# Two transformer layers on one core: one slotted pipeline over both layers in place of two separate ones

## Chip, cores and metric

The kernel runs on one core of one Trainium2 chip. The metric is the device time of one execution in microseconds (us), as the median of several runs. The core has a matrix engine (PE, with its weight loads shown as PEld), a vector engine (DVE), an activation engine (ACT), a general engine (POOL) and a queue for transfers (SP). ACT and POOL can issue transfers too.

## What is computed

Input is x with 16 x 64 = 1024 tokens of 512 features, and a context of the same shape. All is float32. Four residual steps follow one another:

```
x = x + L0_attention(layernorm(x), ctx)      # 32 heads of 128, 8 kv heads, rotary, tanh-capped logits, key mask
x = x + L0_experts(layernorm(x))             # 4 low-rank experts, the best 2 per token, softmax gate
x = x + L1_attention(layernorm(x), ctx)      # 16 heads of 96, 4 kv heads, keys = context and x of the same batch
x = x + L1_linear(layernorm(x))              # x W^T + bias + 16 weighted low-rank updates
```

Attention is within a batch of 64 tokens: a query sees 64 context keys in layer 0, and 64 context plus 64 own keys in layer 1. So a token tile of 128 (two batches) depends on no other tile, except through the weights that all share.

## The kernel before

x stays in eight SBUF tiles xt[0..7] of 128 tokens. hT (L149) holds the context and the normalised x, both transposed, features on the partitions. "Half" means 512 tokens, that is four of the tiles.

`layernorm_T` (L192) normalises all eight tiles in two groups of four: statistics on DVE, square root on ACT, normalising on DVE, four PE transposes a tile into a PSUM tile with tag "pa", and a copy by ACT to hT. It is called four times, ahead of each of the four steps, each time over all tokens.

A layer 0 unit (`l0_unit`, L241) is a kv head and a half. Its **chunks** make the projections: one k chunk (L267), four q chunks (L277), and on every other kv head, in half 0 only, four v chunks for both kv heads and all tokens (L289). A k or q chunk is four matmuls of 128 x 512 (eight PE records, since a float32 matmul shows as two) and then the rotation `rope` (L245): two ACT copies that swap the halves, a product on DVE, one on POOL, a sum on DVE. The projections take PSUM tiles of tag "pa", of which there are two, as the transposes do. Its two **items** are 256 tokens each and go through four stages:

- `l0_scores` (L318): scores on PE, tanh and exp on ACT, mask on POOL (L338, L341)
- `l0_norm` (L346): row sums on PE (sm, L349), reciprocal on DVE (L351), product on POOL (en, L353)
- `l0_av` (L356): weights times values on PE (av, L365), four copies by ACT (at, L374)
- `l0_wo` (L379): two output products on PE (po, L386), each added to a tile xt by DVE (L393)

Layer 1 (`l1_unit`, L510) has the same form: kv head and half, two k chunks (none for the last kv head), three q chunks, eight v chunks for kv head 0, and four items of 128 tokens with the stages `l1_scores` (L581: maximum on DVE, four exponentials on ACT, scaling on POOL), `l1_transpose` (L611: four PE transposes and a DVE copy eT), `l1_av` (L619) and `l1_wo` (L639). Scores, sums and transposes share two PSUM tiles of tag "pb"; av has two of tag "pc", outputs two of tag "pd".

The order is written by `_run_pipeline` (L71), once per layer. In its step n it emits scores of item n, then the second stage of item n-1, the third of n-2, the fourth of n-3, and between these stages the chunks of the next unit, spread over the unit's items. Units follow kv head by kv head, both halves of each. So four items are in work at a time, and a layer's last outputs come three steps after its last scores. The framework that builds the program sets the semaphores and may place ready instructions of an engine in another order than the code's.

Between the two pipelines stands the code of the experts (L440 to L502), with a norm ahead of it and one behind. After the second pipeline come the loads of the last step's weights, their merge (L667 to L674: the low-rank updates multiplied out and added to W), a norm, the bias adds on POOL (L677) and the linear product (pf, L681) with its output transfers.

At the start SP's queue loads the eight x tiles (L145) and then weights, POOL's queue the whole context in one transfer of 2 MB (L150), ACT's queue the small tables. Weight tiles have two buffers per tag; `load_w0` for the next kv head is called with the first chunk of a unit, `load_wo0` after the last.

Of the kernel before, what the change touches and what calls it, by code (L numbers as in the profile page):

```python
# [70 lines left out]
def _run_pipeline(units, lag_stages):  # L71

    n_st = len(lag_stages)
    for f in units[0][0]:
        f()
    flat = [(u, it) for u, (_, items) in enumerate(units) for it in items]  # L80
    states = []
    pending, done_in_unit = [], 0
    for n in range(len(flat) + n_st - 1):
        take = []
        if n < len(flat):
            u, it = flat[n]
            per_unit = len(units[u][1])
            if n % per_unit == 0:
                pending = list(units[u + 1][0]) if u + 1 < len(units) else []
                done_in_unit = 0  # L90
            k = -(-len(pending) // (per_unit - done_in_unit))
            take, pending = pending[:k], pending[k:]
            done_in_unit += 1
            states.append(it)
        cuts = [len(take) * i // n_st for i in range(n_st + 1)]
        spread = [take[cuts[i] : cuts[i + 1]] for i in range(n_st)]
        for s in range(n_st):
            m = n - s
            if 0 <= m < len(flat):
                lag_stages[s](states[m])  # L100
            for f in spread[s]:
                f()
# [3 lines left out]
def two_layer_kernel(  # L106
# [35 lines left out]
    xt = []  # L142
    for i in range(NT):
        t = const.tile([P, D], F32, tag=f"x{i}", name=f"x{i}")
        nc.sync.dma_start(out=t, in_=x[ts(i, P), :])  # L145
        xt.append(t)


    hT = const.tile([P, 2, KC, NTOK], F32, tag="hT", name="hT")  # L149
    nc.gpsimd.dma_start(out=hT[:, 0], in_=ctxT.rearrange("(c p) n -> p c n", p=P))  # L150

    ident = const.tile([P, P], F32, tag="ident", name="ident")
    make_identity(nc, ident)
    blk = const.tile([P, P], F32, tag="blk", name="blk")
    nc.vector.memset(blk, 0.0)
    nc.vector.memset(blk[0:S, 0:S], 1.0)
    nc.vector.memset(blk[S:P, S:P], 1.0)
    eps_c = const.tile([P, 1], F32, tag="eps", name="eps_c")
    nc.vector.memset(eps_c, EPS)
    cos_sb = const.tile([P, S], F32, tag="cos", name="cos_sb")  # L160
    sin_sb = const.tile([P, S], F32, tag="sin", name="sin_sb")
    nc.scalar.dma_start(out=cos_sb, in_=cos)
    nc.scalar.dma_start(out=sin_sb, in_=sin)


    mask_w = const.tile([P, S // 4], I32, tag="mask_w", name="mask_w")
    for j in range(2):
        nc.scalar.dma_start(out=mask_w[j * S : (j + 1) * S, :], in_=maskT)
    keep = const.tile([P, S], F32, tag="keep", name="keep")
    nc.vector.tensor_copy(keep, mask_w.bitcast(U8))  # L170
    cnt = ps.tile([P, S], F32, tag="pb", name="cnt")
    nc.tensor.matmul(cnt, lhsT=blk, rhs=keep, start=True, stop=True)

    none_kept = const.tile([P, S], F32, tag="none_kept", name="none_kept")
    nc.vector.tensor_scalar(none_kept, cnt, 0.0, None, ALU.is_equal)


    tri = const.tile([P, NE, NE], F32, tag="tri", name="tri")
    nc.vector.memset(tri, 0.0)
    for e in range(1, NE):  # L180
        nc.vector.memset(tri[:, e, 0:e], 1.0)

    bias_bc = const.tile([P, D], F32, tag="bias", name="bias_bc")
    nc.scalar.dma_start(out=bias_bc, in_=bias1.partition_broadcast(P))
    w_er = const.tile([P, 2], F32, tag="w_er", name="w_er")
    sc_er = const.tile([P, 2], F32, tag="sc_er", name="sc_er")
    nc.scalar.dma_start(out=w_er, in_=coeffs)
    nc.scalar.dma_start(out=sc_er, in_=scales)
    nc.vector.tensor_mul(w_er, w_er, sc_er)


    def layernorm_T():  # L192
        for grp in range(2):
            tiles = range(grp * 4, grp * 4 + 4)
            mv = small.tile([P, 4, 2], F32, tag="mv", name="mv")
            for n, i in enumerate(tiles):
                st = small.tile([P, 6], F32, tag="st", name="st")
                nc.vector.bn_stats(st, xt[i])
                nc.vector.bn_aggr(mv[:, n, :], st)
            rstd = small.tile([P, 4], F32, tag="rstd", name="rstd")  # L200
            nc.scalar.activation(rstd, mv[:, :, 1], AF.Sqrt, bias=eps_c)
            nc.vector.reciprocal(rstd, rstd)
            for n, i in enumerate(tiles):
                xn = work.tile([P, D], F32, tag="xn", name="xn")
                nc.vector.tensor_scalar(
                    xn, xt[i], mv[:, n, 0:1], rstd[:, n : n + 1], ALU.subtract, ALU.mult
                )
                tp = ps.tile([P, KC, P], F32, tag="pa", name="tp")
                for c in range(KC):
                    nc.tensor.transpose(tp[:, c, :], xn[:, ts(c, P)], ident)  # L210
                nc.scalar.copy(hT[:, 1, :, ts(i, P)], tp)
# [4 lines left out]
    def load_w0(kv):  # L216
        wq = wp.tile([P, KC, G0 * HD0], F32, tag="wq", name="wq")
        nc.sync.dma_start(
            out=wq, in_=wq0[:, ts(kv, G0 * HD0)].rearrange("(c p) n -> p c n", p=P)
        )  # L220
        wk = wp.tile([P, KC, HD0], F32, tag="wk", name="wk")
        nc.sync.dma_start(out=wk, in_=wk0[:, ts(kv, HD0)].rearrange("(c p) n -> p c n", p=P))
        if kv % 2 == 0:
            wv = wp.tile([P, KC, 2 * HD0], F32, tag="wv", name="wv")
            nc.sync.dma_start(
                out=wv, in_=wv0[:, ts(kv // 2, 2 * HD0)].rearrange("(c p) n -> p c n", p=P)
            )
        else:
            wv = w0[kv - 1][2]
        w0[kv] = [wq, wk, wv]  # L230

    def load_wo0(kv):
        wo = wp.tile([P, G0, D], F32, tag="wo", name="wo")
        nc.sync.dma_start(
            out=wo, in_=wo0[ts(kv, G0 * HD0), :].rearrange("(g p) n -> p g n", p=P)
        )
        w0[kv].append(wo)
# [3 lines left out]
    def l0_unit(kv, half):  # L241
# [62 lines left out]
        def first():  # L304
            if half == 0 and kv + 1 < KV0:
                load_w0(kv + 1)
            k_chunk()

        chunks = [first]
        if half == 0 and kv % 2 == 0:  # L310
            chunks += [lambda n=n: v_chunk(n) for n in range(4)]
        chunks += [lambda g=g: q_chunk(g) for g in range(G0)]
        if half == 0:
            chunks.append(lambda: load_wo0(kv))
        items = [{"unit": unit, "quad": qd} for qd in range(2)]
        return chunks, items
# [62 lines left out]
    def l0_wo(it):  # L379
# [14 lines left out]

    load_w0(0)
    layernorm_T()
    _run_pipeline(
        [l0_unit(kv, half) for kv in range(KV0) for half in range(2)],
        [l0_scores, l0_norm, l0_av, l0_wo],
    )  # L400

# [3 lines left out]
    nc.sync.dma_start(out=aw, in_=aw0.rearrange("(c p) n -> p c n", p=P))  # L405
    bcat = const.tile([P, D], F32, tag="bcat", name="bcat")
    for j in range(2):
        nc.sync.dma_start(out=bcat[j * NM : (j + 1) * NM, :], in_=b0)
# [21 lines left out]
    load_w1(0)  # L430
    wv1s = []
    for m in range(2):
        wv = wp.tile([P, 2, KV1 * HD1], F32, tag="wv", name="wv1_sb")
        nc.sync.dma_start(
            out=wv, in_=wv1[ts(m, 2 * P), :].rearrange("(c p) n -> p c n", p=P)
        )
        wv1s.append(wv)
    layernorm_T()

    for grp in range(2):  # L440
# [50 lines left out]
        gmf = gm.rearrange("p n e r -> p (n e r)")  # L491
# [13 lines left out]
    layernorm_T()  # L505
    v1 = [act.tile([P, B // 2, KV1 * HD1], F32, tag="v", name=f"v1_{h}") for h in range(2)]
# [3 lines left out]
    def l1_unit(kv, half):  # L510
# [19 lines left out]
        def first():  # L530
            if half == 0 and kv + 1 < KV1:
                load_w1(kv + 1)
            if kv < PK1:
                unit["k"] = act.tile([HD1, nb, 2, S], F32, tag="k", name="kT1")
            else:
                unit["k"] = k_last[:, half * nb : (half + 1) * nb]
            unit["q"] = act.tile([HD1, nb, G1, S], F32, tag="q", name="qT1")
            if kv < PK1:
                k_chunk(0)
# [37 lines left out]
        if half == 0:  # L577
            chunks.append(lambda: load_wo1(kv))
        return chunks, [{"unit": unit, "pair": pr} for pr in range(nb // 2)]
# [59 lines left out]
    def l1_wo(it):  # L639
# [11 lines left out]
        nc.vector.tensor_add(xt[i], po, xt[i])  # L651

    _run_pipeline(
        [l1_unit(kv, half) for kv in range(KV1) for half in range(2)],
        [l1_scores, l1_transpose, l1_av, l1_wo],
    )

# [73 lines left out]
```

## Time and profile before

| | us |
|---|---|
| median of 3 runs | 1098.24 |
| lowest and highest | 1092.36, 1098.29 |
| the profiled execution | 1091.64 |
| its span in the trace | 1089.9 |
| PE busy | 1053.4 |
| DVE, ACT, POOL busy | 429.3, 318.0, 292.9 |

The span runs from the first to the last recorded instruction; the execution's own time is 1.7 us longer. The stretches between the stages, by the rows of PE in order of time:

| from, to (us) | what PE does |
|---|---|
| 0 to 18.4 | waits for x, apart from one small product |
| 18.4 to 25.9 | first norm's transposes |
| 25.9 to 60.5 | k, v and q of the first unit, k of the second |
| 60.5 to 683.4 | layer 0 items and chunks |
| 683.4 to 690.9 | norm |
| 690.9 to 718.9 | experts |
| 718.9 to 725.9 | norm |
| 725.9 to 1045.8 | layer 1 |
| 1045.8 to 1052.7 | merge |
| 1052.7 to 1061 | norm, with first linear products |
| to 1086.0 | linear; the last output lands near the end of the span |

A busy share is of the whole span. Matmuls are pipelined, so the records of neighbours overlap: 597 ns is the record of one 512-column record, 0.43 us the distance between two. "Idle before" names what the engine waited for last.

### The profile page before, as it was taken

Reading aid. Unit: us, or ns where it says so; the run is one execution under the profiler, and the core shown is the slowest. Engines: PE = TensorE matmul, PEld = TensorE weight load, DVE = VectorE, ACT = ScalarE, POOL = GpSimd, SP = SyncE. Lnnn points to the kernel's source line nnn. Section 1 sums busy time; section 2 is a strip of 40 time slices with the busy share of each in tenths; the row PEclk is TensorE's granted clock in tenths of the full one; section 3 lists DMA queues with packets and bytes.
Section 4 is the critical chain, followed back from the end, with each engine's and each line's share of the span. In section 5 each row is a group of like instructions: output and inputs, shape, how many; then the busy total and the mean of one; then the engine's idle time right before and its main releaser. Section 6 shows DMA issues by size and latency. Waiting matters only on the chain.

```text
span 1089.9 us, 9279 instructions
## 1 busy us (share of the span) xinstructions
PE 1053.4 (97%) x3398; PEld 535.4 (49%) x3398; DVE 429.3 (39%) x639; ACT 318.0 (29%) x835; POOL 292.9 (27%) x257
## 2 busy tenths in 40 slices
PE   3999999999999999999999999789999999999998
PEld 2644455444455444455444444545555555556543
DVE  4145433343433343433344445540123334334661
ACT  2243322232322232222232221231433433333420
POOL 0155422243432243332243341002220111111140
PEclk9999999999999999999999999879999999999999
DMA  9210011011011011011011010000010010010002
GB/s 334 78 42 7 10 39 58 10 39 39 10 39 53 10 39 38 11 39 53 11 29 39 10 58 1 29 0 1 11 49 0 1 59 1 29 39 20 1 1 77
DMA packets 26142, 38.57 MB, mean 35 GB/s; under 512 B 2288, under 2 KB 12528, under 8 KB 26096
## 3 DMA queue, kind: packets, MB, share of 16 engines
q1 hardware_dynamic: 24688, 35.53, 9.8%
q0 software_dynamic: 528, 2.10, 0.5%
q8 instruction: 27, 0.44, 0.2%
q10 hardware_dynamic: 880, 0.34, 0.1%
q14 instruction: 19, 0.16, 0.0%
HBM read 35.87 MB, written 2.10 MB: 35 GB/s over the span
## 4 chain that ended last, share of the span: by engine, by line
PE 95%; DVE 2%; DMA 1%; ACT 1%; issue 0%; POOL 0%; ACTq 0%; DVEq 0%; POOLq 0%
PE pq L280 21%; PE po L386 20%; PE pq L544 8%; PE po L644 7%; PE pv L295 5%; PE pk L272 5%; PE pk L518 4%; PE pv L562 4%; PE av L365 3%; PE sm L349 3%; PE sc L324 3%; PE sc L586 3%; PE av L624 2%; PE pf L681 2%; PE tp L210 1%; PE tp L614 1%
## 5 line engine op out<-in xcount | busy, mean ns | idle before, releaser
L280 PE MATMUL pq<-hT,wq 128*128 128x512 f32 x512 | 231.5, 597 | 0.0
L386 PE MATMUL po<-wo,at 128*128 128x512 f32 x512 | 226.1, 594 | 0.0
L259 POOL TENSOR_TENSOR w<-sh,sin_sb 128x512 f32<-128x512 f32 x80 | 102.7, 1284 | 312.5 <-ACT sh L250 312.2
L386 PEld LDWEIGHTS po<-wo,at 128*128 128x128 f32 x512 | 96.4, 190 | 119.6 <-issue 118.5
L280 PEld LDWEIGHTS pq<-hT,wq 128*128 128x128 f32 x512 | 95.5, 190 | 119.0 <-issue 117.6
L351 DVE RECIPROCAL r<-sm 128x512 f32<-128x512 f32 x32 | 107.4, 3357 | 47.2 <-PE sm L349 44.3
L249 ACT COPY sh<-pq 64x512 f32<-64x512 f32 x64 | 37.2, 582 | 296.2 <-PE pq L280 296.2
L252 DVE TENSOR_TENSOR u<-pq,cos_sb 128x512 f32<-128x512 f32 x64 | 44.0, 688 | 156.4 <-ACT sh L250 156.4
L608 POOL TENSOR_TENSOR e<-e,sm 128x512 f32<-128x512 f32 x32 | 33.2, 1039 | 220.5 <-DVE sm L607 220.5
L393 DVE TENSOR_TENSOR x<-po,x 128x512 f32<-128x512 f32 x64 | 44.2, 690 | 120.5 <-PE po L386 118.1
L644 PE MATMUL po<-wo_sb,at 128*128 128x512 f32 x192 | 87.5, 592 | 0.0
L544 PE MATMUL pq<-hT,wq_sb 128*128 128x512 f32 x192 | 86.0, 592 | 0.0
L338 POOL TENSOR_TENSOR e<-e,keep 128x512 f32<-128x512 f32 x32 | 40.5, 1267 | 92.0 <-ACT e L337 91.7
L265 DVE TENSOR_TENSOR qT<-u,w 128x512 f32<-128x512 f32 x64 | 45.2, 706 | 35.6 <-POOL w L259 35.3
L599 ACT ACTIVATE e<-sc,nmx 128x128 f32<-128x128 f32 x128 | 45.2, 365 | 47.5 <-DVE nmx L595 44.4
L544 PEld LDWEIGHTS pq<-hT,wq_sb 128*128 128x128 f32 x192 | 36.2, 190 | 43.9 <-issue 42.6
L272 PE MATMUL pk<-hT,wk 128*128 128x512 f32 x128 | 57.6, 593 | 0.1
L295 PE MATMUL pv<-wv,hT 128*128 128x256 f32 x256 | 57.2, 380 | 0.0
L353 POOL TENSOR_TENSOR en<-e,r 128x512 f32<-128x512 f32 x32 | 47.5, 1485 | 23.6 <-DVE r L351 15.4
L295 PEld LDWEIGHTS pv<-wv,hT 128*128 128x128 f32 x256 | 48.4, 190 | 10.4 <-issue 3.6
L644 PEld LDWEIGHTS po<-wo_sb,at 128*128 128x128 f32 x192 | 36.3, 190 | 33.8 <-issue 29.9
L552 DVE COPY qT<-pq 96x512 f32<-96x512 f32 x24 | 16.5, 687 | 87.7 <-PE pq L544 87.7
(105 smaller groups left out, 1099.7 us busy)
## 6 DMA issues: line engine op xcount, KB each, us to landing
wq<-in_wq SPq DMA_DIRECT2D x8, 1024.0 KB, 5.5
wo<-in_wo SPq DMA_DIRECT2D x8, 1024.0 KB, 5.3
wq_sb<-in_wq SPq DMA_DIRECT2D x4, 768.0 KB, 4.7
wo_sb<-in_wo SPq DMA_DIRECT2D x4, 768.0 KB, 4.6
x<-in_x SPq DMA_DIRECT2D x8, 256.0 KB, 6.2
hT<-in_ctxT POOLq DMA_DIRECT2D x1, 2048.0 KB, 13.0
wk<-in_wk SPq DMA_DIRECT2D x8, 256.0 KB, 4.1
wv<-in_wv SPq DMA_DIRECT2D x4, 512.0 KB, 5.1
```

The lines of the kernel that those rows point to most:

```text
L259: nc.gpsimd.tensor_tensor(w.rearrange("p (b t) -> p b t", t=S), sh.rearrange("p (b t) -> p b t", t=S), sin_b, ALU.mult,)
L265: nc.vector.tensor_tensor(dst, u, w, ALU.add)
L272: nc.tensor.matmul(pr, lhsT=w0[kv][1][:, c, :], rhs=hT[:, 0, c, tok], start=c == 0, stop=c == KC - 1)
L280: nc.tensor.matmul(pr, lhsT=w0[kv][0][:, c, ts(g, HD0)], rhs=hT[:, 1, c, tok], start=c == 0, stop=c == KC - 1,)
L295: nc.tensor.matmul(pr[:, i, :], lhsT=hT[:, 0, c, ts(2 * n + i, P)], rhs=w0[kv][2][:, c, :], start=c == 0, stop=c == KC - 1,)
L351: nc.vector.reciprocal(r, sm)
L353: nc.gpsimd.tensor_tensor(en.rearrange("p a t -> p (a t)"), ef, r, ALU.mult)
L386: nc.tensor.matmul(po, lhsT=it["at"][:, g, ts(pr, P)], rhs=wo[:, g, :], start=g == 0, stop=g == G0 - 1,)
L393: nc.vector.tensor_add(xt[i], po, xt[i])
L544: nc.tensor.matmul(pr, lhsT=w1s[kv][0][:, c, ts(g, P)], rhs=hT[:, 1, c, ds(half * HALF, HALF)], start=c == 0, stop=c == KC - 1,)
L599: nc.scalar.activation(e[:, n, :], sc[:, n, :], AF.Exp, bias=nmx[:, n : n + 1], scale=SCALE1, accum_out=sm[:, n : n + 1],)
L644: nc.tensor.matmul(po, lhsT=it["at"][:, g].rearrange("d m t -> d (m t)"), rhs=w1s[u["kv"]][2][:, g, :], start=g == 0, stop=g == PK1 - 1,)
```

## The change

`_run_pipeline` goes. `_run(items, fillers)` takes one list of items over both layers and a table of other work by time slot:

```
SLOTS = 4
LAG = 2

def _run(items, fillers):
    last = max([SLOTS * (len(items) - 1) + LAG * 3, *fillers])
    for t in range(last + 1):
        for m in range(len(items)):
            s, odd = divmod(t - SLOTS * m, LAG)
            if not odd and 0 <= s < 4:
                items[m]["stages"][s](items[m])
        for f in fillers.get(t, []):
            f()
```

An item starts every four slots, and its stages are two slots apart: scores at 4m, the second stage at 4m+2, the third at 4m+4, the fourth at 4m+6. In a slot the stages are emitted first, the earlier item ahead, and then the slot's fillers. So at slot 4m stand the third stage of item m-1 and scores of m, at 4m+2 the fourth of m-1 and the second of m.

The order of units is changed so that half 0 ends before half 1, and the chunks of each unit are spread over the slots of the one before (8 slots in layer 0, 16 in layer 1):

```
    units0 = [(kv, half) for kv in range(KV0 - 2) for half in range(2)]
    units0 += [(kv, half) for half in range(2) for kv in (KV0 - 2, KV0 - 1)]
    units1 = [(kv, half) for k2 in range(0, KV1, 2) for half in range(2) for kv in (k2, k2 + 1)]
...
    def spread(a, b, work):
        for n, f in enumerate(work):
            put(a + (b - a) * n // len(work), f)
...
    for a, b in zip(units0, units0[1:]):
        if b != (0, 1):
            spread(begin[0, a], begin[0, b], built0[b][0] + built0[b][1])
```

`layernorm_T` becomes `ln_stats(*tiles)` and `ln_tile(i)`, the experts `experts_mid(grp)` and `experts_out(grp)`, for one half each. They are put at slots counted from the last output of a half:

```
    for half, t in ((0, h0), (1, h1)):
        at = (2, 3, 6, 7, 8) if half == 0 else (2, 4, 8, 9, 11)
        normed = [lambda i=i: ln_tile(i) for i in halves[half]]
        put(t, lambda half=half: ln_stats(*halves[half]))
        put(t + at[0], *normed)
        put(t + at[1], lambda half=half: experts_mid(half))
        put(t + at[2], lambda half=half: experts_out(half))
        put(t + at[3], lambda half=half: ln_stats(*halves[half]))
        put(t + at[4], *normed)
    spread(h0 + 9, u0, built1[0, 0][0])
    spread(u0, begin[1, (1, 0)], built1[1, 0][0])
    spread(h1 + 12, u1, built1[0, 1][0])
    for a, b in zip(units1[2:], units1[3:]):
        spread(begin[1, a], begin[1, b], built1[b][0])
```

With 16 layer 0 units the slots are: half 0 of layer 0 ends at h0 = 114 while units (6, 1) from 112 and (7, 1) from 120 are in work; layer 1 begins at u0 = 128; half 1 ends at h1 = 130; u1 = 160; the last unit begins at 240.

The end of layer 1 is treated in the same way. The merge is cut into four calls `merge(c)`, the linear step into `linear(i)` with the bias add of its tile:

```
    put(begin[1, (2, 0)], load_updates)
    put(begin[1, (2, 1)], load_w, weigh_updates)
    put(begin[1, (3, 1)], *[lambda c=c: merge(c) for c in range(KC)])
    put(h0, lambda: ln_stats(*halves[0]))
    put(begin[1, (3, 1)] + 2, *[lambda i=i: ln_tile(i) for i in halves[0]])
...
    put(h1 - 5, stats(4, 5))
    put(h1 - 4, applied(0), normed(4))
    put(h1 - 3, stats(6), normed(5), applied(1))
    put(h1 - 2, applied(2))
    put(h1 - 1, normed(6), applied(3))
    put(h1, stats(7), applied(4), applied(5), normed(7), applied(6), applied(7))
    _run(items, fillers)
```

The start is rewritten. The context comes in eight transfers on SP's queue (a half is four of 128 x 512), x on ACT's queue, the small tables on POOL's. Weights of the first kv head are loaded in parts, in the order k, v, q:

```
    load_small()
    load_w0(0, 0)
    load_ctx(0)
    load_w0(0, 1)
    for i in range(NT):
        nc.scalar.dma_start(out=xt[i], in_=x[ts(i, P), :])
    load_ctx(1)
    load_w0(0, 2)
    make_identity(nc, ident)
    constants()
    load_wo0(0)
    load_w0(1)
    for f in built0[0, 0][0]:
        f()
    ln_stats(*halves[0])
    for f in built0[0, 1][0]:
        f()
    for i in halves[0]:
        ln_tile(i)
    mask_constants()
    ln_stats(*halves[1])
    for f, i in zip(built0[0, 0][1], halves[1]):
        f()
        ln_tile(i)
    spread(0, begin[0, (0, 1)], built0[0, 1][1])
```

Here built0[u][0] are the k and v chunks of a unit and built0[u][1] its q chunks. The later weight loads become fillers too:

```
    for kv in range(2, KV0):
        put(begin[0, (kv - 1, 0)] - (8 if kv > 2 else 0), lambda kv=kv: load_w0(kv))
    for kv in range(1, KV0):
        put(max(begin[0, (kv, 0)] - 2, 0), lambda kv=kv: load_wo0(kv))
    put(begin[0, (5, 0)], load_experts, load_late)
...
    put(begin[0, (7, 0)], load_wv1)
    put(begin[0, (6, 1)], lambda: load_w1(0))
    put(begin[0, (7, 1)] + 2, lambda: load_w1(1))
    put(begin[0, (7, 1)] + 6, lambda: load_wo1(0))
    put(u0 + 4, lambda: load_wo1(1))
```

The bodies of the chunks and of the stages, the tiles, their buffers and the number of bytes loaded are the same as before.

## The prediction

> **What bounds the kernel now.** I read the busy times first, then the table of windows by stage, then the chain that ended last, then the rows of the two stretches between the layers in order of time.
>
> ```profile
> PE 1053.4 (97%) x3398; PEld 535.4 (49%) x3398; DVE 429.3 (39%) x639; ACT 318.0 (29%) x835; POOL 292.9 (27%) x257
> ...
> PE 95%; DVE 2%; DMA 1%; ACT 1%; issue 0%; POOL 0%; ACTq 0%; DVEq 0%; POOLq 0%
> ```
>
> PE carries the end: 97% busy, 95% of the chain. The windows say where the other 3% lies (columns: length, then busy time of PE, PEld, DVE, ACT and POOL, granted clock, DMA share, GB/s):
>
> ```profile
> 0.00:20.00 20.00, 2.30 (x10) 2.07 (x10) 8.19 (x32) 2.03 (x4) 1.67 (x7) 1.00 0.94 322
> 40.00:640.00 600.00, 600.00 (x1804) 282.32 (x1802) 240.74 (x240) 171.88 (x347) 220.70 (x169) 1.00 0.09 29
> 640.00:720.00 80.00, 67.98 (x246) 34.42 (x246) 45.84 (x100) 16.91 (x37) 10.66 (x9) 0.88 0.08 30
> 720.00:1060.00 340.00, 337.49 (x1199) 190.14 (x1197) 124.15 (x254) 119.46 (x436) 55.95 (x70) 0.99 0.05 17
> ...
> 640.00:650.00 10.00, 8.73 (x28) 3.64 (x28) 5.00 (x5) 1.98 (x5) 5.58 (x5) 1.00 0.21 79
> ...
> 710.00:720.00 10.00, 6.11 (x12) 2.59 (x12) 8.17 (x21) 0.30 (x1) 0.00 (x0) 0.50 0.00 0
> ```
>
> Over 600 us of layer 0 PE has no gap at all, so nothing can be won there and every new wait is paid in full. What can be won is at the ends. I counted PE's work at full pace from undisturbed rows: a chunk of 8 matmul records (q, k, one wo output) takes 3.43 us from start to next start, scores+sums+av of a layer 0 item 3.34, a layer 1 item 4.77 (score to score where no chunk lies between), one token tile's transposes 0.44. Layer 0: (80 chunks + 64 outputs) x 3.43 + 16 v chunks x 3.45 + 32 x 3.34 = 656. Layer 1: 36 chunks x 3.43 + 41.3 of v + 32 x 4.77 = 317. Norm tiles 32 x 0.44 = 14, experts 14.6, merge and linear 80 records x 0.43 = 34. Sum 1036 of the 1089.9 us span; 54 are slack. They lie so. **Head**: the first scores start at 60.49 after 37.9 of work: 22.6. **Middle**: 1.3 before scores at 641.65; first norm (683.4 to 690.9) 7.5 less 3.5 = 4.0; experts (690.9 to 718.9) 28.0 less 14.6 = 13.4, at half clock for most of it; second norm 6.9 less 3.5 = 3.4: together 22. **End**: last norm 2.3, output 3.9. The rest is small.
>
> **The change part by part.** Matmuls, copies, vector work and bytes stay the same in number; order, queues and lags change.
>
> *Head, -6 (2 to 9).* x goes from SP's queue to ACT's; the context, one 2 MB transfer on POOL's queue (13.0 us to landing beside x), becomes eight on SP, the first half behind 0.25 MB of wk. The same table in steps of 2 us sums to 2.7 MB moved by 10 us and 4.3 by 14. With equal shares, the first k chunk has its 1.25 MB when 2.5 have moved, 9.5 us; wv comes at 3.5 MB, 12 us. So v0 starts at 12.5, v0 to v3 and the second k chunk end near 30; four tiles at 0.85 each (their pace in the head, two PSUM buffers behind a 0.59 us copy) 33.5; then four q chunks, each followed by one tile. Both take a buffer of the same pair; a q chunk's is free only 2.1 us after its end (two copies of 0.58, product of 0.69), the tile's 0.8 after its 0.44, so about 0.8 of PE wait per chunk: 4 x 4.7 = 19. Scores near 54 instead of 60.5. The small tables move to POOL's queue (four issues near 1 us), due for the first rotation after 10 us: hidden, and 1 to 2 us late at worst.
>
> *Middle, -19 (12 to 22).* Half 0's norms and experts fall among the last layer 0 units, half 1's among the first layer 1 units. Their waits (copies 0.59, the gate's chain of some 20 short DVE operations, 4.3 us) lie beside items, and the clock should stay up. 22 less some 3 for tiles that queue on the two PSUM buffers.
>
> *End, -2.* Merge and half 0's linear run inside the last unit, so PE has 3 linear tiles (10.3) to cover the last tile's chain: add 0.69, statistics 0.86, square root 0.3, normalising 0.55, transposes, copy, together about 4.6. The 3.9 of output stay. Bias adds (1.27 on POOL) hide beside each 3.43.
>
> *Weight loads, 0.* SP waits in order, each load on the last reader of its buffer. Each is placed behind that reader and about a unit (37 us) ahead of use, against 5.5 us to landing. If one came late, PE would lose up to those 5.5.
>
> *Short lags in layer 0, +40 (0 to 43).* Before, sums and av of an item were a whole item (18 us) apart. Now sums sit at slot 4m+2, av at 4m+4, and a unit without v chunks puts its five chunks at slots 0, 1, 3, 4, 6: one chunk, 3.43, between sums and av. The chain is shown here (start, duration, engine, line, operation, in brackets idle before):
>
> ```profile
> 638.19 1.14 PE L365 MATMUL av<-en,v 64*128 64x256 f32 x8
> ...
> 639.26 1.13 PE L386 MATMUL po<-wo,at 128*128 128x512 f32 x2
> ...
> 641.65 1.08 PE L324 MATMUL sc<-qT,kT 128*64 128x256 f32 x8 [1.27 <-DVE qT L265]
> ...
> 642.67 1.13 PE L349 MATMUL sm<-e,blk 128*128 128x512 f32 x2
> ...
> 643.63 6.17 PE L386 MATMUL po<-wo,at 128*128 128x512 f32 x14
> ...
> 643.83 3.36 DVE L351 RECIPROCAL r<-sm 128x512 f32<-128x512 f32 x1 [2.23 <-PE sm L349]
> ...
> 647.27 1.26 POOL L353 TENSOR_TENSOR en<-e,r 128x512 f32<-128x512 f32 x1 [0.54 <-DVE r L351]
> ```
>
> Sums start at 642.67, en is ready at 648.53: 5.86, and 6.2 where POOL's en takes its usual 1.58. PE has 0.96 + 3.43 = 4.39 to do. So av waits 1.5 to 1.8, say 1.65, and behind it in PE's queue stand the next scores, the next chunk and wo. Of 32 items, six have v chunks beside them (two chunks, 6.9) and the last two layer 1's first chunks: 24 x 1.65 = 40. The lower bound is 0, because PE's order isn't the code's:
>
> ```profile
> 56.94 3.60 PE L272 MATMUL pk<-hT,wk 128*128 128x512 f32 x8
> 60.49 1.08 PE L324 MATMUL sc<-qT,kT 128*64 128x256 f32 x8
> ```
>
> The code emits these scores ahead of this k chunk; the program was built with the chunk first, since q's rotation wasn't ready. If the builder foresees the reciprocal's 3.36 as well, it slips the next scores and a matmul or two in. No row shows that. The nearest row is the 1.27 above: same layer, a 3.4 us chain, and the built order still came 1.27 too early. The chain here is 5.1 behind the sums; I take the full 1.65.
>
> *Short lags in layer 1, +5 (0 to 38), table loads, +3.* Scores to transposes takes 5.2 to 6.0 (maximum 0.69, four exponentials 1.5, scaling on POOL 1.04); with no chunk in that half of an item PE has scores and wo, 3.46. In code order ten items would wait 1.75 or more and fourteen would wait 1.2 for the transposed copy: 35 to 38. Here rows do show the builder filling in (scores, a piece of a k chunk, scores, at 763.8), and what stayed was 0.60, 0.19 and 0.24 in the last items:
>
> ```profile
> 1030.28 1.06 PE L586 MATMUL sc<-k_last,qT 96*128 96x128 f32 x8
> ...
> 1036.30 0.66 PE L614 MATMUL tp<-ident,e 128*128 128x128 f32 x4 [0.24 <-POOL e L608]
> ```
>
> I take 0.35 at some 15 handoffs. Norms between items make square root and exponential alternate: about 8 more table loads. The row has 1283 ns for one, and the next ACTIVATE 1.30 after its start. [...] Three pairs fall where layer 1's chain has little cover: 3 x 2.6 = 7.7 by the row[...]. [...] count 3 because chunks cover the rest.
>
> *Clock under many short waits, 0.* [...] 710 to 720, waits near 3 us, clock 0.50; 640 to 650, one wait of 1.27, clock 1.00. By the row 24 waits cost nothing more[...]. I take the row.
>
> **Sum.** 1089.9 - 6 - 19 - 2 + 40 + 5 + 3 = 1111 span. The profiled run was 1091.64, 1.7 above its span; the median of the runs, 1098.24, is 6.6 above that, the lowest 1092.36 near it. I add 1.7 and 1.5: 1114.
>
> **Rivals.** *The order hides the lags, faster.* One mechanism, at sums to av: the next scores (0.97) and two matmuls of the next chunk (1.7) go ahead of av. Then 1089.9 - 27 + 4 = 1067 span, 1070 with what lies around it. For it: 56.94 above, and no PE gap in 600 us. Against: 641.65. It decides when the wait per item is under 0.6. *Gain given back, no change.* The builder covers half: 20 instead of 40, giving 1091 span, 1094. For it: waits of 0.2 to 0.6 in layer 1's tail. *The change doesn't do what it says*: the middle stays a gap because half 1's chain (some 35 us) runs out of other work; but the first two layer 1 units hold 38 us of items and 17 of chunks, so this loses at most a few us, and ends within the other cases.
>
> **How the numbers follow.** Paid lags 0.45 (1106 to 1124), half covered 0.24 (1084 to 1104), covered 0.31 (1064 to 1082). Layer 1 at its upper bound is inside the first one's top. The range 1068 to 1124 leaves out the fringes. 1% is about what a measurement of this kernel tells from no change; the cases fall on its sides, so slower 0.45, within 0.24, faster 0.31.
>
> **What would show it.** Right: PE's waits list av L365 <- POOL en some 24 times at 1.5 to 1.8, PE below 600 in layer 0's 600 us, the stretch between the layers without a clock drop, first scores near 54. Wrong: PE still gapless in layer 0 with scores or half chunks between sums and av; or head and middle keeping their slack; or the clock falling below 1.00 among the items.

## The result and the profile after

The changed kernel takes 1128.86 us (median of 4 runs, 1124.95 to 1128.89) against 1095.3 us of the kernel before (4 runs, 1091.26 to 1098.29): 1.030 times as long, 95% interval 1.025 to 1.035. It is slower, as forecast, but lies beyond the forecast's upper end of 1124. The profiled execution spans 1127.0 us, 37.1 more than before.

From the page of the changed kernel, first the busy times, then the chain that ended last:

```profile
PE 1062.4 (94%) x3398; PEld 533.3 (47%) x3398; DVE 434.8 (39%) x641; ACT 324.9 (29%) x843; POOL 287.0 (25%) x263
...
PE 77%; DVE 9%; POOL 6%; ACT 4%; issue 3%; DMA 1%; POOLq 0%; ACTq 0%; DVEq 0%
```

PE has the same 3398 records, but no longer the chain: 95% before, 77% now. VectorE and GpSimd, 2% of the old chain together, carry 15%: their chains are no longer covered. The windows by stage of the changed kernel say where (columns as before: length, busy PE, PEld, DVE, ACT, POOL, granted clock, DMA share, GB/s):

```profile
0.00:20.00 20.00, 10.64 (x30) 5.67 (x31) 9.35 (x31) 3.09 (x6) 5.83 (x14) 1.00 0.93 322
40.00:640.00 600.00, 568.38 (x1698) 269.13 (x1697) 227.76 (x224) 159.51 (x325) 195.44 (x155) 1.00 0.08 26
640.00:720.00 80.00, 73.51 (x222) 33.09 (x221) 42.26 (x66) 21.20 (x41) 22.55 (x19) 0.89 0.08 24
720.00:1060.00 340.00, 334.25 (x1188) 182.94 (x1187) 125.79 (x261) 118.94 (x403) 49.98 (x65) 1.00 0.07 21
```

PE starts earlier (10.6 us of work in the first 20 against 2.3), but the 600 us from 40 to 640, gapless before, now hold 568.4; about 6 of the 31.6 that are missing lie ahead of the first scores at 65.80, the rest in layer 0. And from 640 to 720 the clock is 0.89, as low as before (0.88), though the old gap between the layers is full of work.

For the account I laid both traces out alike: the length of a stretch less PE's work in it at full pace, with the paces the prediction used. This is loss, by idling or by half clock. The count works with mean paces, so a line is good to about 1.5 us.

| stretch | loss before | loss after | change | forecast |
|---|---|---|---|---|
| head, to the first scores | 21.5 | 25.5 | +4.0 | -6 |
| layer 0, to the first norm between the layers | 2.7 | 33.5 | +30.8 | +40 |
| between the layers, to the last norm tile of half 1 | 24.1 | 21.4 | -2.7 | -19 |
| layer 1 | -0.9 | 2.1 | +3.0 | +5 and +3 |
| end, from about the last unit | 6.6 | 10.1 | +3.5 | -2 |

The changes sum to 38.6, where the spans differ by 37.1; the 1.5 between them is the error of the count, since both traces hold the same 3398 records, kind by kind. PE's waits in the changed kernel (us in total, times, longest):

```profile
PE sc L318 <- DVE qT L266: 14.7, 15, 1.3
PE av L359 <- POOL en L347: 12.9, 22, 2.1
PE pk L273 <- DMA hT<-in_ctxT: 7.1, 3, 6.2
PE pq L281 <- ACT hT L203: 6.6, 5, 1.5
```

Only the first was in the list before, with 1.3 us. The forecast had named the second, as 24 waits of 1.5 to 1.8. One unit of layer 0 in the changed kernel, in order of time, shows both:

```profile
129.71 1.02 PE L343 MATMUL sm<-e,blk 128*128 128x512 f32 x2
130.57 3.60 PE L281 MATMUL pq<-hT,wq 128*128 128x512 f32 x8
134.00 1.02 PE L273 MATMUL pk<-hT,wk 128*128 128x512 f32 x2
135.59 1.13 PE L359 MATMUL av<-en,v 64*128 64x256 f32 x8 [0.56 <-POOL en L347]
137.55 1.08 PE L318 MATMUL sc<-qT,kT 128*64 128x256 f32 x8 [0.83 <-DVE qT L266]
```

Between sums and av stand the one chunk of the forecast and a first piece of the next unit's k chunk (x2), which the builder pulled forward; av still comes 0.56 early. The chunk is the unit's last query chunk. It ends at 134.1, its rotated result is ready at 137.49, and the next unit's scores need it: they wait another 0.83. In the first item of the same unit the wait at av is 0.42. Together 1.81 per unit; from sums to sums two items on it is 39.8 us against some 37.6 of work at full pace. (The waits cost a little more than their brackets say: run 1 below, which has none here, takes 37.4.)

### The profile page after: what moved, and what is told of

Read it like the earlier page. It is cut to its first block, busy times and chain, and to the rows that moved or that the text cites. A ratio compares the mean times of both kernels' runs of the same rounds, so it can differ in the third digit from the quotient of the medians.

```text
span 1127.0 us, 9305 instructions
## 1 busy us (share of the span) xinstructions
PE 1062.4 (94%) x3398; PEld 533.3 (47%) x3398; DVE 434.8 (39%) x641; ACT 324.9 (29%) x843; POOL 287.0 (25%) x263
## 4 chain that ended last, share of the span: by engine, by line
PE 77%; DVE 9%; POOL 6%; ACT 4%; issue 3%; DMA 1%; POOLq 0%; ACTq 0%; DVEq 0%
PE po L380 20%; PE pq L281 12%; PE pq L537 7%; DVE r L345 6%; PE po L636 6%; PE pk L511 4%; PE pv L555 4%; PE pv L296 4%; PE pk L273 3%; PE sc L318 3%; PE sm L343 3%; PE pf L681 2%; POOL en L347 2%; PE sc L578 2%; PE av L616 2%
## 5 line engine op out<-in xcount | busy, mean ns | idle before, releaser
L281 PE MATMUL pq<-hT,wq 128*128 128x512 f32 x512 | 234.1, 602 | 6.6 <-ACT hT L203 6.6
L347 POOL TENSOR_TENSOR en<-e,r 128x512 f32<-128x512 f32 x32 | 40.9, 1279 | 285.6 <-DVE r L345 255.9
L537 PE MATMUL pq<-hT,wq_sb 128*128 128x512 f32 x192 | 88.9, 593 | 0.0
L273 PE MATMUL pk<-hT,wk 128*128 128x512 f32 x128 | 64.1, 622 | 7.1 <-DMA hT<-in_ctxT 7.1
L318 PE MATMUL sc<-qT,kT 128*64 128x256 f32 x256 | 42.8, 402 | 14.7 <-DVE qT L266 14.7
L368 ACT COPY at<-av 128x256 f32<-128x256 f32 x128 | 38.4, 387 | 37.4 <-PE av L359 37.3
```

The source lines that it names most:

```text
L273: nc.tensor.matmul(pr, lhsT=w0[kv][1][:, c, :], rhs=hT[:, 0, c, tok], start=c == 0, stop=c == KC - 1)
L281: nc.tensor.matmul(pr, lhsT=w0[kv][0][:, c, ts(g, HD0)], rhs=hT[:, 1, c, tok], start=c == 0, stop=c == KC - 1,)
L318: nc.tensor.matmul(sc[j * S : (j + 1) * S, pr, :], lhsT=k[:, tok], rhs=q[:, :, tok], start=True, stop=True,)
L347: nc.gpsimd.tensor_tensor(en.rearrange("p a t -> p (a t)"), ef, r, ALU.mult)
L537: nc.tensor.matmul(pr, lhsT=w1s[kv][0][:, c, ts(g, P)], rhs=hT[:, 1, c, ds(half * HALF, HALF)], start=c == 0, stop=c == KC - 1,)
```

## Experiments

**1. Layer 0's chunks at other slots.** Theory A: thin cover at the two handoffs, sums to av and last query chunk to scores. Theory B: interleaving as such. Number and lags stay, places change: of a unit's five chunks two come between sums and av of each item, and the last query chunk an item before its scores.

```diff
-        if b != (0, 1):
-            spread(begin[0, a], begin[0, b], built0[b][0] + built0[b][1])
+        chunks = built0[b][0] + built0[b][1]
+        if b == (7, 1):
+            spread(begin[0, a], begin[0, b], chunks)
+        elif b != (0, 1):
+            at = (-2, -1, 2, 3, 4) if len(chunks) == 5 else (-2, -1, 0, 1, 2, 2, 3, 4, 5)
+            for n, f in zip(at, chunks):
+                put(begin[0, a] + n, f)
```

(The first unit's second half gets its four query chunks at slots 0, 2, 3, 4.)

> Layer 0's projection chunks of the changed kernel keep their number and their lags, but stand elsewhere: of five, two lie between the sums and the context matmuls of the first item, two in those of the second, and the last query chunk comes an item before the scores that read it. Theory A (the 30 us that layer 0 lost are thin cover at these two handoffs, where one chunk of 3.44 us stands against a chain of about 4.8 us from sums to context matmul, and none but the context matmuls against 3.4 us from query chunk to scores): the waits "sc <- DVE qT" (14.7 us) and "av <- POOL en" (12.9 us) all but vanish in the stretch from the first scores to 660 us, its loss falls from about 30 to about 5 us, and the time falls by 20 to 25 us to about 1105. Theory B (the loss is that projections are cut up between attention items at all: changes of shape, more switches, other engines in the way): the waits move to other instructions, and the time stays within 6 us of the changed kernel's 1129.

Measured: 1095.97 us, 33 less than the changed kernel where A said 20 to 25, and 1.003 times the kernel before (interval 1.001 to 1.005). Layer 0's loss fell from 33.5 to 4.2; from 100 to 630 us neither handoff waits, but for one 0.8 at av. Of the rest, 2.5 is the head, whose first query chunk had its full clock in this execution (below). The window and one unit:

```profile
40.00:640.00 600.00, 589.39 (x1785) 280.69 (x1784) 245.50 (x246) 165.45 (x340) 204.98 (x162) 1.00 0.09 28
```

```profile
126.42 1.02 PE L343 MATMUL sm<-e,blk 128*128 128x512 f32 x2
127.28 3.60 PE L273 MATMUL pk<-hT,wk 128*128 128x512 f32 x8
130.71 3.60 PE L281 MATMUL pq<-hT,wq 128*128 128x512 f32 x8
134.24 1.13 PE L359 MATMUL av<-en,v 64*128 64x256 f32 x8
135.30 1.08 PE L318 MATMUL sc<-qT,kT 128*64 128x256 f32 x8
```

Two chunks between sums and av, no bracket behind any line, no piece of a chunk pulled ahead. Theory A holds, B falls: chunks stand between attention items here too.

**2. One lag put back.** For the first 24 items av comes four slots behind the sums instead of two, the output at eight.

```diff
-            s, odd = divmod(t - SLOTS * m, LAG)
-            if not odd and 0 <= s < 4:
-                items[m]["stages"][s](items[m])
+            lags = (0, 2, 6, 8) if m < 24 else (0, 2, 4, 6)
+            if t - SLOTS * m in lags:
+                items[m]["stages"][lags.index(t - SLOTS * m)](items[m])
```

> The changed kernel with one of its three lags put back for the first 24 items alone: the context matmuls come four slots behind the sums in place of two, and the output matmuls follow at eight; chunks stay in their slots. Now a chunk and eight output matmuls (10.3 us) lie between the sums and the context matmuls, and eight output matmuls between the last query chunk and the next scores, while between scores and sums one chunk and the context matmuls (4.5 us) stand against a chain of about 4.6 us. Theory A (thin cover from short lags): layer 0's loss falls from about 30 to 5 to 9 us, time about 1105 to 1109. Theory B (interleaving itself): within 6 us of 1129. Theory C (the short lag is right and only the query chunk's place is wrong): the wait before the scores goes, the loss falls by no more than half, about 1114.

Measured: 1103.7 us, 1.007 times the kernel before (1.003 to 1.011). Layer 0's loss is 11.9, a little over A's 5 to 9. The order it makes:

```profile
119.20 1.12 PE L343 MATMUL sm<-e,blk 128*128 128x512 f32 x2
120.16 3.60 PE L281 MATMUL pq<-hT,wq 128*128 128x512 f32 x8
123.60 7.03 PE L380 MATMUL po<-wo,at 128*128 128x512 f32 x16
130.56 1.08 PE L318 MATMUL sc<-qT,kT 128*64 128x256 f32 x8
```

A chunk and an item's output matmuls, 10.3 us, now cover both chains. So lag and place are two ways to the same cover, and C falls with B. What is left of the 11.9 lies in the first items (2.4 before the first av, 1.9 before the first sums, and an estimated 1.7 because the clock stood at 0.50 from 80.2 to 83.6 us, behind the wait at av) and in the passage back to short lags.

**3. The reciprocal in halves.** Is one wait only the other's shadow?

```diff
-        nc.vector.reciprocal(r, sm)
         en = work.tile([P, 2, G0 * S], F32, tag="en", name="en")
-        nc.gpsimd.tensor_tensor(en.rearrange("p a t -> p (a t)"), ef, r, ALU.mult)
+        for h in range(2):
+            part = ds(h * 256, 256)
+            nc.vector.reciprocal(r[:, part], sm[:, part])
+            nc.gpsimd.tensor_tensor(en[:, h, :], ef[:, part], r[:, part], ALU.mult)
```

> The changed kernel with the reciprocal of the sums and the multiplication behind it each cut into two halves of 256 columns, so that the second half of one runs beside the first of the other; the chain from sums to context matmul becomes about 0.6 us shorter, the order of the chunks stays. Theory A1 (the two waits of a unit share one stretch: behind the last query chunk the scores can't start before 3.4 us are over, whoever fills them): the wait "av <- POOL en" goes nearly everywhere, but at the second item of each unit what it gives back is taken by "sc <- DVE qT", which grows from 14.7 to about 20 us; the time falls by 5 to 6 us. Theory A2 (the waits are independent and add up): "av <- POOL en" falls by some 10 us, "sc <- DVE qT" stays at 14.7, the time falls by about 10 us. Theory B (thin cover doesn't matter): no change, or longer by the fixed cost of the two instructions more per item.

Measured: 1120.04 us, 8.8 less by the medians; but these stand at different mean clocks. At 0.989 its span is 1120.9 and the changed kernel's 1127.0, so 6.1 less; at 0.992 it is 1118.2 against 1123.1, 4.9 less. PE's waits:

```profile
PE sc L318 <- DVE qT L266: 14.9, 15, 1.9
...
PE av L361 <- POOL en L349: 6.0, 22, 1.8
```

The total is A1's, the lists fit neither: the wait at av fell by 6.9 and the one at the scores did not grow. In order of time one sees why: the piece of the k chunk that stood ahead of av now stands behind it, and fills what av gave back. The gain came from the first item of each unit, as A1 has it: from its sums to the next ones it is 17.34 us now instead of 17.93, while the second item's step stayed at 21.84. The two instructions more cost little: both halves of the reciprocal take 3.37 where it took 3.36, and the two products 0.73 each where the one in the unit above took 1.26. The longer wait, for the rotated queries, is untouched by a shorter chain from sums to av.

**4. The head in another order.** First the unit's four query chunks, then half 1's tiles.

```diff
-    for f, i in zip(built0[0, 0][1], halves[1]):
-        f()
-        ln_tile(i)
+    for f in built0[0, 0][1]:
+        f()
+    for i in halves[1]:
+        ln_tile(i)
```

> In the head of the changed kernel the four query chunks of the first unit are built one after the other and the four tiles of the second half are normalised behind them, in place of chunk and tile in turn. Theory A (the 1.49 us waits of each chunk for a tile's copy, which stands on ScalarE behind the two copies of the chunk before, make the head late): four such waits go, 6 us, and tiles wait for each other by 0.5 to 0.8 us each, so that the time falls by 3 to 6 us; the first query chunk at half clock stays as it is, for nothing ahead of it changes. Theory B (these waits only stand where the head would wait for rotated queries anyway): the first scores come as late as before, and the time moves by less than 1.5 us.

Measured: 1121.45 us, 7.4 less, a little over A's 3 to 6. The first scores start at 58.32 instead of 65.80; the head's loss is 20.5 instead of 25.5, and 1.9 more went in the first items of layer 0. Theory A holds. The lines of the changed kernel, then of this one:

```profile
38.89 6.19 PE L281 MATMUL pq<-hT,wq 128*128 128x512 f32 x8 [0.67 <-ACT hT L203]
...
47.02 3.70 PE L281 MATMUL pq<-hT,wq 128*128 128x512 f32 x8 [1.49 <-ACT hT L203]
```

```profile
38.41 16.52 PE L281 MATMUL pq<-hT,wq 128*128 128x512 f32 x32 [0.68 <-ACT hT L203]
```

In turn, each chunk waits 1.49 for the tile before it, whose copy (0.59) stands on ScalarE behind the two copies (0.58 each) of the chunk before that. In a row, four chunks run without a wait. The other thing to read: 6.19 for a chunk whose like takes 3.70. The clock was at 0.50 there; in this run it cost 2.7 of the 16.52 too.

**5. Filling the two waits between the layers.** Here the changed kernel waits twice within 3.7 us, and then everything runs at half pace until 716.4 (16 records of output matmuls, the last part of them at full clock again, take 9.65 instead of 7.03):

```profile
697.07 1.13 PE L359 MATMUL av<-en,v 64*128 64x256 f32 x8 [1.42 <-POOL en L347]
699.36 1.97 PE L318 MATMUL sc<-qT,kT 128*64 128x256 f32 x8 [1.16 <-DVE qT L266]
...
711.27 9.65 PE L380 MATMUL po<-wo,at 128*128 128x512 f32 x16
```

```profile
680.00:700.00 20.00, 15.92 (x75) 9.36 (x75) 10.31 (x23) 4.23 (x10) 5.28 (x6) 0.98 0.11 40
700.00:718.00 18.00, 16.76 (x30) 5.55 (x27) 9.12 (x14) 3.08 (x5) 3.79 (x3) 0.55 0.00 0
```

```diff
+    def busy():
+        pd = ps.tile([P, D], F32, tag="pa", name="pz")
+        for g in range(3):
+            nc.tensor.matmul(pd, lhsT=blk, rhs=bcat, start=g == 0, stop=g == 2)
+        nc.vector.tensor_copy(scrap, pd[:, 0:1])
+
+    put(119, busy)
```

> The changed kernel with three matmuls more that nothing needs (128x512, 2.6 us of TensorE in all), put between a query chunk and the context matmuls at 697 us, where TensorE waited 1.42 us and then 1.16 us and its granted clock fell to half for some 18 us behind it. The output is the same. Theory A (the waits of a few us in a row take the clock down, and the half clock costs 8 to 9 us): with the waits filled the granted clock stays at 1.00 from 697 to 718, and the time falls by 7 to 9 us although work is added. Theory B (the clock falls for something else, such as the 64-row matmuls of the experts): it falls all the same, and the time is the same or up to 1 us longer.

Measured: 1121.09 us, 7.8 less with 2.6 us of work more. From 700 to 720 the clock was 1.00, and the stretch's loss fell from 21.4 to 12.6 (the three matmuls are counted as work). Theory A.

```profile
700.00:720.00 20.00, 18.05 (x62) 7.97 (x62) 11.91 (x20) 5.93 (x13) 4.70 (x5) 1.00 0.12 39
```

**6. The same waits filled with work that is due anyway.** Item 28's output matmuls are emitted one slot later.

```diff
-            s, odd = divmod(t - SLOTS * m, LAG)
-            if not odd and 0 <= s < 4:
-                items[m]["stages"][s](items[m])
+            lags = (0, 2, 4, 7) if m == 28 else (0, 2, 4, 6)
+            if t - SLOTS * m in lags:
+                items[m]["stages"][lags.index(t - SLOTS * m)](items[m])
```

> The changed kernel with one item's output matmuls (those of item 28, ready long before) emitted one slot later, behind the sums of the next item, so that TensorE has them in reserve while the middle's two waits of 1.42 and 1.16 us at 697 to 699 us stand; no work is added. Theory A (short waits close together take the clock down): both waits go, 2.6 us, and the granted clock stays at 1.00 from 697 to 718, which gives 8 to 9 us more: 10 to 12 us less in all. Theory B (the three added matmuls of the other run happened to keep the clock up by being dense 512-column work, the waits are not the point): the waits go and the clock still falls: 2 to 3 us less.

Measured: 1118.11 us, 10.8 less; the stretch's loss is 12.9. Both waits are gone. The window of this kernel (the program is some 6 us further on there):

```profile
700.00:718.00 18.00, 17.61 (x61) 8.41 (x61) 8.91 (x15) 4.71 (x11) 2.17 (x3) 1.00 0.12 44
```

Clock 1.00, and 61 records in 18 us instead of 30, though not all of the same kinds. No added dense work was needed, so theory B falls. The profiled execution is 12.6 shorter; 3.2 of that is the head, where its first query chunk had the full clock.

**7. The end.** The linears of tiles 0 to 2 are emitted between the last unit's items.

```diff
-    put(h1 - 4, applied(0), normed(4))
-    put(h1 - 3, stats(6), normed(5), applied(1))
-    put(h1 - 2, applied(2))
+    put(h1 - 12, applied(0))
+    put(h1 - 8, applied(1))
+    put(h1 - 5, applied(2))
+    put(h1 - 4, normed(4))
+    put(h1 - 3, stats(6), normed(5))
```

> The changed kernel with the last linear of tiles 0, 1 and 2 emitted earlier, between the last unit's items (8, 5 and 3 slots sooner), where TensorE waits 0.91, 1.54, 0.98 and 0.71 us for copies and normalised scores; tile 3 and the second half stay. Theory A (the end is short of cover since all four merges are emitted at the start of the last unit, and the linears of the first half in a block behind its last items): of the 10 us that the stretch from the first merge to the end loses, 3 to 4 go. Theory B (the linears are needed as cover for the last four tiles' statistics and transposes): the waits come back there, and the time stays within 1 us.

Measured: 1121.69 us; at equal mean clock (0.989) its spans are 1121.5 and 1121.7 against 1127.0, so 5.4 less; the end's loss is 5.5 instead of 10.1. Theory A. This run's profile brought something else. Its stretch between the layers is the changed kernel's, wait by wait, and yet the clock stayed up:

```profile
694.25 1.14 PE L359 MATMUL av<-en,v 64*128 64x256 f32 x8 [1.42 <-POOL en L347]
696.54 1.08 PE L318 MATMUL sc<-qT,kT 128*64 128x256 f32 x8 [1.16 <-DVE qT L266]
```

So the same waits stood ahead of a fall in one execution and of none in another. The mean clock of single executions counts it roughly: 17 us at half clock are 0.008 of the span, and a fall in the head (6.8 us) is another 0.003. Among the 39 executions of the changed kernel and of runs 1, 2, 4 and 7, which keep both waits, 30 show 0.994 or less and 9 more than that. Among the 12 of runs 5, 6 and 8, which fill them, none is below 0.995. Run 3, where the two waits became 0.20 and 1.85 us, lost the clock too, for 13.7 us.

The times of the clock's changes show a step. In the changed kernel they come at 37.11, 43.94, 699.30 and 716.36, so 6.83, 655.36 and 17.06 us apart, which is 2, 192 and 5 times 3.413; the two of the kernel before, at 700.68 and 724.57, are 7 times 3.413 apart. So I divide the time of one execution into stretches of that length, counted from a change. Here are the last stretch before the fall and the half clock behind it in the changed kernel, then the two stretches that the same waits fall into in run 7:

```profile
695.89:699.30 3.41, 1.13 (x8) 0.69 (x8) 1.38 (x2) 2.08 (x6) 3.35 (x4) 1.00 0.48 177
699.30:716.36 17.06, 15.76 (x26) 5.24 (x27) 8.65 (x14) 3.13 (x6) 2.92 (x4) 0.50 0.03 11
```

```profile
691.57:694.98 3.41, 1.99 (x9) 0.88 (x9) 1.91 (x2) 1.16 (x2) 2.05 (x3) 1.00 0.08 20
694.98:698.40 3.42, 1.85 (x14) 0.68 (x10) 0.69 (x1) 1.93 (x6) 1.70 (x2) 1.00 0.56 210
```

In the changed kernel nearly all of both waits lies in one stretch, and PE is busy for 1.13 us of it; in run 7 a border passes between them, at 694.98, and PE is busy for 1.99 and 1.85 us. Three more stretches side with this. Half clock followed one with 1.02 us of busy PE (697.27 to 700.68 in the kernel before) and one with 1.09 (33.70 to 37.11 in the changed kernel); full clock followed one with 1.54 (78.07 to 81.49 in the changed kernel, with most of a wait of 2.08 at the first av). No limit between them is shown. The two waits are the same in both executions, their place against the borders is not.

**8. All repairs together**: the edits of runs 1, 4, 6 and 7 in one kernel.

> The three repairs and the head's new order in one kernel: layer 0's chunks moved as in the first run, the first unit's query chunks ahead of the second half's tiles, item 28's output matmuls a slot later, the linears of tiles 0 to 2 earlier. If the four losses are apart from each other, it takes from the changed kernel 30 (layer 0), 5 (head), 10 (middle) and 3 (end) us: about 1079, range 1074 to 1086, faster than the kernel before by some 1.2 %. If they only push one wait into the next, or if the clock falls elsewhere, it stays at 1090 to 1096, no faster than the kernel before.

Measured: 1077.57 us, 0.987 times the kernel before (interval 0.983 to 0.990), 51 us less than the changed kernel. Losses in the five stretches: 20.7, 2.2, 14.0, 2.0, 5.2. Its windows, and two stretches of 3.41 us from the middle:

```profile
40.00:640.00 600.00, 594.73 (x1800) 283.28 (x1799) 246.09 (x250) 169.15 (x346) 205.98 (x163) 1.00 0.09 28
640.00:720.00 80.00, 76.00 (x256) 39.43 (x255) 30.57 (x52) 22.04 (x45) 21.31 (x29) 0.98 0.07 20
...
641.27:644.69 3.42, 1.43 (x4) 0.44 (x3) 2.14 (x2) 1.69 (x3) 3.34 (x3) 1.00 0.00 0
644.69:648.10 3.41, 3.41 (x11) 2.38 (x10) 2.91 (x2) 1.17 (x2) 0.47 (x1) 0.50 0.00 0
```

The four losses were apart from each other; the sum of the four repairs came within 1.5 us of what was expected of it. This version beats both kernels, the one before by 1.3%. The clock is not quite clear in it: one wait of 1.99 us for masked scores lies within a single stretch, with 1.43 us of busy PE, and the next runs at 0.50. In run 6 a wait of the same length lay across a border, with 2.83 and 2.01 us of busy PE on its two sides, and the clock stayed at 1.00.

## Why the forecast was right in sign and short in size

**Short lags in layer 0, +40: the mechanism right, its size and half of its place wrong.** Measured +30.8. The step took 24 waits of 1.65 at one handoff. That one took 11.5 in layer 0's listed waits, and another that was put at nothing took 13.5, so that the sum came near 40 is in part luck. The builder did pull scores or a piece of a chunk ahead, which the step allowed for and then didn't count, so av waits 0.42 to 0.56. But the pulled work doesn't help the second handoff. A chain of 3.4 us runs from the last query chunk to the next scores, and before, it was the single 1.27 in the list; the short lag put that chunk right ahead of av and scores. The step used that 1.27 as a sign of what the builder does and did not ask which items would have the same neighbour now. Runs 1 and 2 show that cover at these two places is nearly the whole of it, run 3 that they are two.

**Middle, -19: wrong, and the largest miss.** Measured -2.7. The step said that the waits lie beside items and "the clock should stay up". It fell, behind the two waits that the av and scores of layer 0's last items brought into the stretch. Runs 5 and 6 price that: about 9 of the 16 us missed. Some 7 of these 9 are the clock: run 7's profile keeps the waits without the fall, and its stretch from the first norm tile to the last one of half 1 is 7.1 us shorter. With the clock up some 12.8 are still lost where the step left 3: 7.4 of listed waits in run 6, the largest 2.0 for masked scores, 1.6 for the experts' additions, 1.2 for a transpose buffer held by a query copy, and small gaps for the rest.

**Clock under many short waits, 0: right where it was asked, wrong where it was not.** In layer 0 all those waits left the clock at 1.00, as the row taken said. Those waits stand alone or in twos of 1.4 us in all, with 17 us of dense work between the pairs. (In runs 2 and 3 the longer wait before the first av, 2.09 and 1.80 us, stood ahead of 3.4 us at 0.50; in the changed kernel one of 2.08 left the clock at 1.00.) The row was read as "waits of 1.3 are harmless", and the two ends were not asked for waits close together. In the head 1.43 and 0.92 within 3.4 us stood ahead of 6.8 us at 0.50; in the middle 1.42 and 1.16 within 3.7 us ahead of 17.1 us of it. What followed the same waits went with how many of them fell into one stretch of 3.413 us (1.13 us busy and a fall, 1.99 and 1.85 and none).

**Head, -6: wrong, +4.0.** v0 started at 15.07 instead of 12.5, since the second context transfers and wv landed later than equal shares gave: PE waited 6.24, 0.40 and 0.41 for pieces of the context and 1.83 for wv. A chunk waits 1.49, not 0.8: the step left out that the tile's copy stands in ScalarE's queue behind the two copies of the chunk (46.38 behind 45.18 and 45.77). Late v0 is 2.6, the longer waits 4 x 0.7 = 2.8, the half clock 2.7, and the rest of the 10 lies in half 0's tiles, which wait 1.43, 0.92 and 0.67. Run 4 shows the order to be the cause of the chunks' waits.

**End, -2: wrong, +3.5.** The linears did cover the last tiles, as the step says. What it didn't count: the last unit has no projection left, so its own items wait (1.54, 0.98, 0.91, 0.71) while half 0's linears stand behind them all. Run 7 gives 4.6 back.

**Layer 1, +5 and table loads +3: right in kind.** Measured +3.0 for both. There are 13 table loads instead of 7, each 1283 ns as before; what part of the 3.0 is theirs was not separated. **Weight loads, 0: right**; PE waits for no weight but wv at 1.8, though SP itself waits for PE up to 63.8 us at a time.

Head, middle and end came out 10 + 16.3 + 5.5 worse than their terms, the lags 9.2 + 5 better; less the 1.5 by which the count is off that is +16, the distance from 1111 to 1127. Of the rivals, the second was half right: at sums to av the builder covered more than half. Its time did not come, because the handoff that it did not price took the rest.

## What to carry to other kernels

When a pipeline's lags are shortened, list for every producer and consumer pair what work lies between them in the order that will be built, and the chain's length beside it; here 3.4 us of work against 4.8 and next to none against 3.4 cost 31 us, and moving chunks, with nothing else changed, gave 29 of them back. Waits of up to a microsecond were cheap here when they came to 1.4 us together, with some 17 us of dense work behind them (0.56 and 0.83 in the unit shown, clock 1.00), and dear when they came to 2.6 us within 3.7: behind 1.42 and 1.16 us the changed kernel's clock was at 0.50 for 17.1 us, and scores of 1.08 took 1.97. Work that is due anyway, held back by one slot, was the cheapest filler: run 6 took 10.8 us off with it, run 5, with 2.6 us of work more, 7.8.

## What was not expected of the hardware

Behind two waits of 1.42 and 1.16 us, with 1.13 us of work between them, TensorE's granted clock was at 0.50 for 17.1 us, at a cost of about 7 us beyond the waits; in run 8, behind a single wait of 1.99 us, for 3.4. Once down, it stayed down through three stretches of 3.413 us in which PE stood as busy without a gap (706.13 to 716.36 in the changed kernel), where in the head it was back at 1.00 behind one such stretch (40.53 to 43.94); why, no run here shows. The falls looked at went with how little of one stretch of 3.413 us PE was busy (1.02 to 1.43 us), not with the longest wait: one of 2.08 us, with 1.54 us of busy PE in its stretch, left the clock at 1.00. And where the borders of these stretches lie against the program was not the same in two executions: at 695.89 and 699.30, around both waits, in the changed kernel, and at 694.98, between them, in run 7. More than one time was measured for a kernel with such places: 1114.48 us at a mean clock of 0.999 and 1123.48 at 0.989, both for run 7. In the head, likewise, the first query chunk took 6.19 us in the changed kernel and 3.70 in run 1, behind the same waits: in the changed kernel the stretch before it held 1.09 us of busy PE, in run 1 the two stretches there held 2.22 and 1.72.
